# A fused Swin block and dynamic convolution: where operands are zeroed, who scales fc1, and the order of the first steps

## The chip, the cores and the metric

The kernel runs on one core of one Trainium2 chip. The metric is the device time in microseconds (us) of one execution, the median of several. Five engines work side by side, each through its own list of instructions in order: TensorE (PE in the profile, with its weight loads as PEld), VectorE (DVE), ScalarE (ACT), GpSimd (POOL) and SyncE (SP), which here only issues transfers. They wait for one another through semaphores. Transfers (DMA) are issued from the queues of SP, ACT and POOL.

## The reference, cut to what matters

The input is `x` (16, 192, 56, 56) in float32. Two layers follow each other. The first is a shifted-window attention block with an MLP, the second a depthwise 3x3 convolution whose taps are computed from the mean of its input.

```python
shortcut = x
h = _ln(transpose(x), norm1_g, norm1_b)          # over the 192 channels
h = roll(h, (-3, -3)); win = windows_7x7(h)      # 64 windows of 49 tokens an image
q, k, v = win @ qkv_w + qkv_b                    # 6 heads of 32
attn = softmax(q * SCALE @ k + rel_bias[REL_IDX] + mask)
out = attn @ v @ proj_w + proj_b
x1 = shortcut + unroll(out)
y = _ln(x1, norm2_g, norm2_b)
y = gelu(y @ fc1_w + fc1_b) @ fc2_w + fc2_b
x  = x1 + y                                      # end of layer 0
t  = relu(batchnorm(mean(x) @ w1.T))             # layer 1
wt = (t @ w2.T + b2) * MASK                      # only 4 of the 9 taps are left by MASK
out = depthwise_conv3x3(x, wt) + bias
```

## The kernel before

An image is worked on in four steps of two rows of windows each, so there are 64 steps (`NS`). A steady loop runs attention of step i, the MLP of step i - 2 and pieces of the convolution of finished images. Ahead of the loop stands a hand-ordered prologue (`manual_schedule`: each engine's instructions stand in the order in which the code emits them), which loads the weights, folds the norms' scale and mean into them, zeroes the padded operands and takes the attention of the first two steps. The change lies in this prologue alone. PSUM is used as four pairs of banks, taken with `banks(name, k)`.

The helpers that it touches:

```python
def columns(rows, n, name, k, copy):                 # rows of parameters to columns
    nc.vector.tensor_copy(rows[:, DIM:256], rows[:, C0:DIM])
    ...                                              # two transposes on TensorE, then copy()

def fold_scale(raw, g, dst, groups):                 # weight rows times the norm's gain
    for to, lo, n, factor in groups:
        for c in range(2):
            d, r = dst[:, c, to : to + n], raw[:, c, lo : lo + n]
            if factor == 1.0:
                nc.vector.tensor_scalar(d, r, g[c], None, ALU.mult)
            else:
                nc.vector.tensor_scalar(d, r, g[c], factor, ALU.mult, ALU.mult)

def shift(dst, raw, n, be, name):                    # the norm's offset through the weights
    ...
    row = one.tile([1, 2, n // 2], F32, tag="o", name=name)
    nc.scalar.copy(row, dst[0:1, :, : n // 2])

def norm_vars(keys, st, tag="dev"):                  # part = mean of squares - mean^2
    d = one.tile([128, T], F32, tag=tag, ...)
    nc.scalar.activation(part, st[lo:hi, 0, :T], AF.Square)
    nc.vector.tensor_tensor(part, st[64 + lo : 64 + hi, 0, :T], part, ALU.subtract)

def attention_qk(i, kq, ke, kk, between=None, evac=nc.scalar):
    for m in (0, 2, 1):
        short(dsts[m], ...)          # narrow products: 64 channels, win1
    if between:
        between()
    for m in (0, 1, 2):
        long(dsts[m], ...)           # wide products: 128 channels, win0
    ...
```

The prologue, cut to what the change and the prediction speak of:

```python
nc.vector.memset(rel_r, 0.0)
rows3 = columns_load(((norm2_g, 1), ...), "yn1", "cols2", nc.gpsimd)   # 5 DMAs of GpSimd
nc.sync.dma_start(mask_t, win_mask)                  # 113 partitions, last of SP's first loads
for j in range(2):
    for yq in range(WS):
        nc.gpsimd.dma_start(rel_r[...], ...)         # 14 DMAs of GpSimd
nc.gpsimd.memset(win0, 0.0)
nc.gpsimd.memset(win1, 0.0)
...
g1, be1, bq, bk, bv = columns(*rows1, 2, nc.vector.tensor_copy)
norm_squares("1_0", 0, 0, nc.scalar, ("yn0", "q4"))
fold_scale(raw, g1, wqkv, (...))                     # qkv, on VectorE
st = banks("st_a", 3); norm_stats(...)
part, _ = norm_vars(keys, st, "o")                   # tile of tag "o"
norm_root(part); nc.vector.reciprocal(part, part)
norm_squares("1_1", 1, 0, nc.scalar)
pm = fold_means(wqkv, 3 * DIM, "fq", 0)
row = shift(pq, raw, 3 * DIM, be1, "qkb_row")        # tile of tag "o" too
norm_squares("1_2", 2, 1, nc.scalar)
...                                                  # dv_0 (TensorE), fold_center, turn_row
g2, be2, f2b, pb, cb = columns(*rows3, 1, nc.scalar.copy)
norm1_scale(0, pd[:, :, :T], nc.vector)              # writes win0, win1
...
biases(0, 0)                                         # reads rel_r and mask_t, on VectorE
nc.gpsimd.memset(kbd, 0.0)
for t in vbd: nc.gpsimd.memset(t, 0.0)
for t in prob: nc.gpsimd.memset(t, 0.0)
st = banks("st_b", 0); norm_stats(...)
part, _ = norm_vars(keys, st); norm_root(part)
table(AF.Exp)
biases(0, 1)
...
qs[0], outs = attention_qk(0, 1, 2, 3)
pvs, v_rest, v_whole = attention_v(0, (0, 1))
for f in outs: f()
fold_scale(rawf, g2, wf1, ((0, 0, HID, 1.0),))       # fc1
attention_v_out(pvs)                                 # vbd, half on VectorE, half on ScalarE
norm1_scale(1, dvs.pop(0), nc.gpsimd)
...
norm1_scale(2, dvs.pop(1), nc.gpsimd)
pm = fold_means(wf1, HID, "ff", 1)                   # bank pair 1
top(2)
residual(0, pp, pair1)
norm_squares("2_0", 0, 1, nc.scalar)
st = banks("st_c", 0)
norm_stats(keys, {0: 3, 1: 0}, st)
qs[2], outs = attention_qk(2, 2, 1, 3, None, nc.vector)   # pe in bank pair 1
share(1)
fold_center(wf1, HID, pm)                            # reads bank pair 1
...
prts = [attention_turn(1, wp, (2, 3)[wp % 2]) for wp in range(4)]
```

Of the kernel before, what the change touches and what calls it, by code (L numbers as in the profile page):

```python
# [8 lines left out]
F32 = mybir.dt.float32  # L9
AF = mybir.ActivationFunctionType  # L10
# [26 lines left out]
def tile_swin_then_dynamic_conv(  # L37
# [112 lines left out]

    def fold_scale(raw, g, dst, groups):
        for to, lo, n, factor in groups:
            for c in range(2):
                d, r = dst[:, c, to : to + n], raw[:, c, lo : lo + n]
                if factor == 1.0:
                    nc.vector.tensor_scalar(d, r, g[c], None, ALU.mult)
                else:
                    nc.vector.tensor_scalar(d, r, g[c], factor, ALU.mult, ALU.mult)
# [15 lines left out]
    def shift(dst, raw, n, be, name):  # L174


        for c in range(2):
            cs = slice(c * n // 2, (c + 1) * n // 2)
            mm(dst[:, c, : n // 2], be[0].broadcast_to([128, 128]), raw[:, 0, cs], True, False)
            mm(  # L180
                dst[:, c, : n // 2],
                be[1][0:64].broadcast_to([64, 128]),
                raw[0:64, 1, cs],
                False,
                True,
            )
        row = one.tile([1, 2, n // 2], F32, tag="o", name=name)
        nc.scalar.copy(row, dst[0:1, :, : n // 2])
        return row.rearrange("o c n -> o (c n)")
# [65 lines left out]
    def table(func):  # L255

        nc.scalar.activation(junk, eps_t[0:1], func)  # L257
# [17 lines left out]
    def norm_folded(key, i, side):  # L275
# [11 lines left out]

        def sums():
            for p, h in own:
                nc.gpsimd.tensor_tensor(xs[p, 0], v0[p, h], v1[p], ALU.add)  # L290
            nc.gpsimd.tensor_tensor(xs[:, 0], xs[:, 0], xs[:, 1], ALU.add)

# [590 lines left out]
    side = 2 * WS - 1  # L883
    for j in range(2):
        for yq in range(WS):
            q = j * 64 + yq * WS
            nc.gpsimd.dma_start(
                rel_r[q : q + WS].rearrange("p (y x) h -> p y (x h)", y=WS),
# [4 lines left out]
                ),  # L893
            )
    nc.gpsimd.memset(win0, 0.0)
    nc.gpsimd.memset(win1, 0.0)
    rel_hk = rel_r[:, ::-1, :].rearrange("p k h -> p h k")

    def biases(r, e):
# [14 lines left out]

    g1, be1, bq, bk, bv = columns(*rows1, 2, nc.vector.tensor_copy)
    norm_squares("1_0", 0, 0, nc.scalar, ("yn0", "q4"))
    fold_scale(
        raw,
# [45 lines left out]
    biases(0, 0)  # L964
    nc.gpsimd.memset(kbd, 0.0)
    for t in vbd:
        nc.gpsimd.memset(t, 0.0)
    for t in prob:
        nc.gpsimd.memset(t, 0.0)

# [30 lines left out]
    for f in outs:  # L1001
        f()
    fold_scale(rawf, g2, wf1, ((0, 0, HID, 1.0),))
    attention_v_out(pvs)
    norm1_scale(1, dvs.pop(0), nc.gpsimd)
    w2v = w2.rearrange("(c t) r -> c t r", t=9)[:, 0:NTAP, :]
# [71 lines left out]
    keys = {0: "1_3", 1: "2_0"}  # L1078
    norm_stats(keys, {0: 3, 1: 0}, st)
    qs[2], outs = attention_qk(2, 2, 1, 3, None, nc.vector)  # L1080
    share(1)
# [4 lines left out]
    part, _ = norm_vars(keys, st)  # L1086
    table(AF.Sqrt)
    norm_root(part)

    s, m, g, b = (bn[:, k] for k in range(4))  # L1090
    nc.scalar.activation(s, s, AF.Sqrt, bias=eps_t)
    nc.vector.reciprocal(part, part)
    dvs.update(norm_spread(keys, part))
    outs[0]()
    outs[1]()
    prts = [attention_turn(1, wp, (2, 3)[wp % 2]) for wp in range(4)]
    outs[2]()
# [8 lines left out]
    table(AF.Gelu)  # L1106
    sums_()
    yns[0] = norm2_scale(0, dvs.pop(1), True)
    fold()
    attention_v_out(pvs)  # L1110
# [245 lines left out]
```

## Time and profile before

| What | Value |
|---|---|
| Device time, median of three | 3050.23 us (3049.95 to 3051.91) |
| Span of the profiled execution | 3046.8 us |
| TensorE busy | 3021.9 us (99%) |
| VectorE busy | 2156.5 us (71%) |
| ScalarE busy | 1947.1 us (64%) |
| GpSimd busy | 1345.4 us (44%) |
| TensorE busy in 0 to 100 us | 87.6 us |
| TensorE busy in 100 to 300 us | 200.0 us |

The busy time of TensorE is that between start and modelled end of its matmuls, so it says where TensorE had something in hand and not how well it was used. The last two rows come from the table of stretches of 20 us; they tell the prologue from the loop. The lines that the prediction reads are shown there.

### The profile page before, as it was taken

Reading aid. Unit: us, or ns where it says so; the run is one execution under the profiler, and the core shown is the slowest. Engines: PE = TensorE matmul, PEld = TensorE weight load, DVE = VectorE, ACT = ScalarE, POOL = GpSimd, SP = SyncE. Lnnn points to the kernel's source line nnn. Section 1 sums busy time; section 2 is a strip of 40 time slices with the busy share of each in tenths; the row PEclk is TensorE's granted clock in tenths of the full one; section 3 lists DMA queues with packets and bytes.
Section 4 is the critical chain, followed back from the end, with each engine's and each line's share of the span. In section 5 each row is a group of like instructions: output and inputs, shape, how many; then the busy total and the mean of one; then the engine's idle time right before and its main releaser. Section 6 shows DMA issues by size and latency. Waiting matters only on the chain.

```text
span 3046.8 us, 62149 instructions
## 1 busy us (share of the span) xinstructions
PE 3021.9 (99%) x25174; PEld 1892.6 (62%) x25174; DVE 2156.5 (71%) x3840; ACT 1947.1 (64%) x3159; POOL 1345.4 (44%) x1270
## 2 busy tenths in 40 slices
PE   8999999999999999999999999999999999999998
PEld 5666666666666666666666666666666666666654
DVE  8666676676676676766866767767767668667664
ACT  4665676676666666766756667667666666666563
POOL 6434544434435345444444354453444444543422
PEclk9999999999999999999999999999999999999999
DMA  4102121121211112121121211212111121111101
GB/s 111 33 31 59 41 68 45 42 65 44 75 38 62 52 44 67 39 78 35 42 67 47 70 36 52 65 41 77 39 44 59 46 73 38 62 52 43 33 30 56
DMA packets 68710, 159.87 MB, mean 52 GB/s; under 512 B 11250, under 2 KB 35288, under 8 KB 66504
## 3 DMA queue, kind: packets, MB, share of 16 engines
q1 hardware_dynamic: 66766, 153.84, 16.6%
q8 instruction: 198, 3.24, 0.4%
q0 software_dynamic: 1360, 1.26, 0.3%
q14 instruction: 88, 0.72, 0.1%
q10 hardware_dynamic: 298, 0.81, 0.1%
HBM read 92.24 MB, written 38.93 MB: 43 GB/s over the span
## 4 chain that ended last, share of the span: by engine, by line
PE 97%; DVE 1%; POOL 1%; DMA 0%; issue 0%; ACT 0%; POOLq 0%; DVEq 0%; ACTq 0%
PE ph L87 26%; PE pf L87 25%; PE pv L87 8%; PE pp L87 8%; PE po L87 6%; PE pq L87 5%; PE pt L575 5%; PE sc L87 4%; PE pk L87 4%; PE pe L87 4%; PE st L87 2%; PE pc L87 0%; DVE e L553 0%; DVE bias_t L905 0%; PE pb_p L87 0%
## 5 line engine op out<-in xcount | busy, mean ns | idle before, releaser
L87 PE MATMUL pf<-hid,wf 128*128 128x392 f32 (+1 forms) x3072 | 802.7, 494 | 1.5 <-DVE e L546 1.5
L87 PE MATMUL ph<-yn,wf 128*128 128x392 f32 (+1 forms) x3072 | 799.1, 497 | 0.3 <-DVE x L651 0.3
L562 POOL TENSOR_TENSOR prob<-e,tot 113x588 f32<-113x588 f32 x256 | 298.2, 1176 | 1096.8 <-DVE tot L561 1096.7
L87 PEld LDWEIGHTS ph<-yn,wf 128*128 128x128 f32 (+1 forms) x3072 | 427.0, 188 | 344.1 <-issue 46.9
L87 PEld LDWEIGHTS pf<-hid,wf 128*128 128x128 f32 (+1 forms) x3072 | 386.9, 164 | 300.7 <-issue 119.8
L518 ACT COPY vbd<-pv 49x192 f32<-49x192 f32 x512 | 160.1, 313 | 576.7 <-DVE vbd L518 572.2
L711 DVE SCALAR_TENSOR_TENSOR x<-pf,cols,x 128x784 f32<-128x784 f32 (+1 forms) x128 | 106.2, 830 | 507.2 <-PE pf L87 453.3
L665 ACT ACTIVATE hid<-ph,f1b 128x784 f32<-128x784 f32 x384 | 336.8, 913 | 134.1 <-PE ph L87 132.6
L775 DVE SCALAR_TENSOR_TENSOR y<-x,wt,y 128x770 f32<-128x770 f32 x282 | 287.3, 1028 | 15.3 <-ACT y L767 7.0
L87 PEld LDWEIGHTS pv<-wqkv,win 64*128 64x128 f32 (+1 forms) x2048 | 255.5, 189 | 30.7 <-issue 1.2
L87 PE MATMUL pv<-wqkv,win 64*128 64x192 f32 (+1 forms) x2048 | 272.2, 325 | 0.0
L553 DVE TENSOR_TENSOR e<-e,top 113x588 f32<-113x588 f32 x256 | 261.7, 1022 | 8.9
L290 POOL TENSOR_TENSOR xs<-x,x 64x392 f32<-64x392 f32 x246 | 249.0, 1012 | 34.7 <-DVE x L651 25.5
L87 PE MATMUL pp<-o,wp 128*128 128x392 f32 (+2 forms) x896 | 251.4, 514 | 0.0
L581 ACT COPY prt<-pt 128x678 f32<-128x678 f32 x256 | 179.2, 726 | 111.3 <-PE pt L575 109.8
L257 ACT ACT_TABLE_LOAD x192 | 246.3, 1283 | 5.2 <-issue 1.8
L556 ACT ACTIVATE e<-e 113x588 f32<-113x588 f32 x256 | 177.1, 692 | 110.9 <-DVE e L553 110.9
L546 DVE TENSOR_TENSOR e<-sc,bias_t 113x588 f32<-113x588 f32 x256 | 179.4, 762 | 60.7 <-PE sc L87 59.7
L411 POOL TENSOR_TENSOR yn<-x,dv 128x784 f32<-128x784 f32 x62 | 116.1, 1872 | 234.6 <-DMA dv<-rows 234.6
L575 PEld LDWEIGHTS pt<-ident,prob 113*128 113x128 f32 x1536 | 165.5, 141 | 65.5 <-issue 36.3
L87 PE MATMUL po<-prt,vbd 128*64 128x49 f32 x6144 | 197.1, 224 | 0.5 <-ACT prt L581 0.5
L87 PEld LDWEIGHTS po<-prt,vbd 128*64 128x64 f32 x6144 | 188.9, 138 | 9.7 <-ACT prt L581 0.6
(185 smaller groups left out, 4440.1 us busy)
## 6 DMA issues: line engine op xcount, KB each, us to landing
dv<-rows SPq DMA_DIRECT2D x127, 392.0 KB
xs<-x SPq DMA_DIRECT2D x246, 98.0 KB
x<-in_x_dram SPq DMA_DIRECT2D x15, 1484.0 KB
out_dram<-y SPq DMA_DIRECT2D x46, 392.0 KB
out_dram<-y SPq DMA_DIRECT2D x48, 196.0 KB
x<-in_x_dram SPq DMA_DIRECT2D x15, 392.0 KB
x<-in_x_dram SPq DMA_DIRECT2D x15, 350.0 KB
out_dram<-y SPq DMA_DIRECT2D x16, 308.0 KB
```

The costliest lines, as they stand in the source:

```text
L87: nc.tensor.matmul(dst, lhs, rhs, start=start, stop=stop, skip_group_check=True)
L257: nc.scalar.activation(junk, eps_t[0:1], func)
L290: nc.gpsimd.tensor_tensor(xs[p, 0], v0[p, h], v1[p], ALU.add)
L518: copy(dst, src[s * 64 : s * 64 + N, h, :, :, j, :])
L546: nc.vector.tensor_tensor(e, sc[:PW, :, : HEADS * N], rel, ALU.add)
L553: nc.vector.tensor_tensor(ehs[wp], ehs[wp], t.broadcast_to([PW, 2 * HEADS, N]), ALU.subtract)
L556: nc.scalar.activation(es[wp], es[wp], AF.Exp)
L562: nc.gpsimd.tensor_tensor(prob[wp][:PW, :, 0:N], ehs[wp], t.broadcast_to([PW, 2 * HEADS, N]), ALU.mult)
L575: nc.tensor.transpose(pt[:, a, g * PW : (g + 1) * PW], prob[wp][:PW, h : h + 2, :].rearrange("p h k -> p (h k)"), ident[:PW, :PW],)
L581: nc.scalar.copy(prt, pt[:, :, : 3 * PW])
L665: nc.scalar.activation(hid[:, f], phs[f][:, :, :T], AF.Gelu, bias=f1b[:, f : f + 1])
L775: nc.vector.scalar_tensor_tensor(dst, src, wt[:, kc, t : t + 1], dst, ALU.mult, ALU.add)
```

## The change

Six things are moved, and no arithmetic of the result is changed.

1. The zero fills leave their place behind `biases(0, 0)`. `prob` and `vbd` are zeroed on GpSimd directly behind its first transfers; `kbd` is zeroed on VectorE, in the stretch in which that engine waits for the qkv weights.
2. The fourteen loads of the relative bias table are divided: seven stay on GpSimd's queue, behind the fills of `win0` and `win1`, and seven go to ScalarE's queue, behind the squares of step 0.
3. The row in which the shifted offsets are collected uses the buffer of tag "xs" and no longer that of tag "o", which holds the deviations at that time.
4. fc1 is scaled on ScalarE by an activation with a per-partition scale, behind the evacuation of V and not ahead of it.
5. In step 2, the statistics (`st_c`) are put between the narrow and the wide products of Q, K and E; the root follows the evacuation of Q.
6. In step 1, the turned probabilities use the bank pairs 2 and 0, where they used 2 and 3, and the root of the batch norm moves behind them. The sums of step 4's folded norm are divided, with the second norm's scaling between them.

```diff
--- before.py
+++ after.py
@@ -148,11 +148,13 @@
 
 
 
-    def fold_scale(raw, g, dst, groups):
+    def fold_scale(raw, g, dst, groups, engine=nc.vector):
         for to, lo, n, factor in groups:
             for c in range(2):
                 d, r = dst[:, c, to : to + n], raw[:, c, lo : lo + n]
-                if factor == 1.0:
+                if engine is nc.scalar:
+                    nc.scalar.activation(d, r, AF.Copy, scale=g[c])
+                elif factor == 1.0:
                     nc.vector.tensor_scalar(d, r, g[c], None, ALU.mult)
                 else:
                     nc.vector.tensor_scalar(d, r, g[c], factor, ALU.mult, ALU.mult)
@@ -184,7 +186,7 @@
                 False,
                 True,
             )
-        row = one.tile([1, 2, n // 2], F32, tag="o", name=name)
+        row = one.tile([1, 2, n // 2], F32, tag="xs", name=name)
         nc.scalar.copy(row, dst[0:1, :, : n // 2])
         return row.rearrange("o c n -> o (c n)")
 
@@ -285,10 +287,12 @@
             nc.sync.dma_start(xs[0:64, 1], v0[64:128, 0])
             nc.sync.dma_start(xs[64:128, 1], v0[0:64, 1])
 
-        def sums():
-            for p, h in own:
-                nc.gpsimd.tensor_tensor(xs[p, 0], v0[p, h], v1[p], ALU.add)
-            nc.gpsimd.tensor_tensor(xs[:, 0], xs[:, 0], xs[:, 1], ALU.add)
+        def sums(parts=(0, 1)):
+            if 0 in parts:
+                for p, h in own:
+                    nc.gpsimd.tensor_tensor(xs[p, 0], v0[p, h], v1[p], ALU.add)
+            if 1 in parts:
+                nc.gpsimd.tensor_tensor(xs[:, 0], xs[:, 0], xs[:, 1], ALU.add)
 
         def squares(engine):
             def those_of(dst, src):
@@ -881,10 +885,11 @@
     nc.sync.dma_start(mask_t, win_mask)
 
     side = 2 * WS - 1
-    for j in range(2):
+
+    def rel_load(j, queue):
         for yq in range(WS):
             q = j * 64 + yq * WS
-            nc.gpsimd.dma_start(
+            queue.dma_start(
                 rel_r[q : q + WS].rearrange("p (y x) h -> p y (x h)", y=WS),
                 bass.AP(
                     rel_bias.tensor,
@@ -892,8 +897,12 @@
                     [[HEADS, WS], [side * HEADS, WS], [1, WS * HEADS]],
                 ),
             )
+
     nc.gpsimd.memset(win0, 0.0)
     nc.gpsimd.memset(win1, 0.0)
+    rel_load(0, nc.gpsimd)
+    for t in (*prob, *vbd):
+        nc.gpsimd.memset(t, 0.0)
     rel_hk = rel_r[:, ::-1, :].rearrange("p k h -> p h k")
 
     def biases(r, e):
@@ -913,7 +922,9 @@
 
 
     g1, be1, bq, bk, bv = columns(*rows1, 2, nc.vector.tensor_copy)
+    nc.vector.memset(kbd, 0.0)
     norm_squares("1_0", 0, 0, nc.scalar, ("yn0", "q4"))
+    rel_load(1, nc.scalar)
     fold_scale(
         raw,
         g1,
@@ -962,11 +973,6 @@
     nc.vector.tensor_scalar(qkb[0:64, 2:3], qkb[0:64, 2:3], SCALE, None, ALU.mult)
     nc.vector.tensor_scalar(kb, pick, qkb[:, 1:2], None, ALU.mult)
     biases(0, 0)
-    nc.gpsimd.memset(kbd, 0.0)
-    for t in vbd:
-        nc.gpsimd.memset(t, 0.0)
-    for t in prob:
-        nc.gpsimd.memset(t, 0.0)
 
 
     st = banks("st_b", 0)
@@ -1000,8 +1006,8 @@
     v_whole()
     for f in outs:
         f()
-    fold_scale(rawf, g2, wf1, ((0, 0, HID, 1.0),))
     attention_v_out(pvs)
+    fold_scale(rawf, g2, wf1, ((0, 0, HID, 1.0),), nc.scalar)
     norm1_scale(1, dvs.pop(0), nc.gpsimd)
     w2v = w2.rearrange("(c t) r -> c t r", t=9)[:, 0:NTAP, :]
     b2v = b2.rearrange("(c t) -> c t", t=9)[:, 0:NTAP]
@@ -1076,8 +1082,9 @@
     norm_squares("2_0", 0, 1, nc.scalar)
     st = banks("st_c", 0)
     keys = {0: "1_3", 1: "2_0"}
-    norm_stats(keys, {0: 3, 1: 0}, st)
-    qs[2], outs = attention_qk(2, 2, 1, 3, None, nc.vector)
+    qs[2], outs = attention_qk(
+        2, 2, 1, 3, lambda: norm_stats(keys, {0: 3, 1: 0}, st), nc.vector
+    )
     share(1)
     fold_center(wf1, HID, pm)
     top(3)
@@ -1085,15 +1092,15 @@
     share(3)
     part, _ = norm_vars(keys, st)
     table(AF.Sqrt)
+    outs[0]()
     norm_root(part)
+    nc.vector.reciprocal(part, part)
+    dvs.update(norm_spread(keys, part))
+    outs[1]()
+    prts = [attention_turn(1, wp, (2, 0)[wp % 2]) for wp in range(4)]
 
     s, m, g, b = (bn[:, k] for k in range(4))
     nc.scalar.activation(s, s, AF.Sqrt, bias=eps_t)
-    nc.vector.reciprocal(part, part)
-    dvs.update(norm_spread(keys, part))
-    outs[0]()
-    outs[1]()
-    prts = [attention_turn(1, wp, (2, 3)[wp % 2]) for wp in range(4)]
     outs[2]()
     outs[3]()
     o = attention_rows(1, attention_values(1, prts, 2, 3))
@@ -1104,8 +1111,9 @@
     copies()
     squares(nc.scalar)()
     table(AF.Gelu)
-    sums_()
+    sums_((0,))
     yns[0] = norm2_scale(0, dvs.pop(1), True)
+    sums_((1,))
     fold()
     attention_v_out(pvs)
     pp, pair1, p_narrow, p_rest, p_whole = project(1, o, 3, 2)
```

## The prediction

> **What bounds the kernel now.** I read the page first: TensorE's busy time, then the chain that ended last.
>
> ```profile
> PE 3021.9 (99%) x25174; PEld 1892.6 (62%) x25174; DVE 2156.5 (71%) x3840; ACT 1947.1 (64%) x3159; POOL 1345.4 (44%) x1270
> PE 97%; DVE 1%; POOL 1%; DMA 0%; issue 0%; ACT 0%; POOLq 0%; DVEq 0%; ACTq 0%
> ```
>
> TensorE is the bound, and the table of stretches says where it is not: busy 87.6 us of the first 100, then 200.0 of the next 200. The change touches the prologue alone, so at most the 12.4 idle us, plus matmuls that run at a low clock, are to be had. TensorE is full from about 100 us on, so a prologue that is shorter by d should end the kernel d earlier; what other engines save counts only as far as it moves TensorE. I then read the timeline of each engine over 0 to 100 us. The longest hole of TensorE after its start, and what lies behind it, in the timelines of VectorE, GpSimd and TensorE (start, duration, engine, line, what; in brackets the idle time before):
>
> ```profile
> 16.02 6.42 DVE L138 COPY cols_rows<-cols_rows 5x64 f32<-5x64 f32 x1
> 17.02 5.42 DVE L387 TENSOR_TENSOR win<-x,dv 128x343 f32<-128x343 f32 x2
> ```
>
> ```profile
> 13.60 0.97 POOL L895 MEMSET win<- 128x1024 f32 x1
> 14.49 0.54 POOL L896 MEMSET win<- 128x512 f32 x1
> 14.96 2.08 POOL L965 MEMSET kbd<- 128x2352 f32 x1
> 16.95 2.72 POOL L967 MEMSET vbd<- 128x1536 f32 x2
> 19.59 2.80 POOL L969 MEMSET prob<- 128x768 f32 x4
> ```
>
> ```profile
> 22.50 0.26 PE L141 MATMUL cols_p<-ident,cols_rows 5*128 5x5 f32 x1 [3.35 <-DVE win L395]
> 22.69 0.87 PE L87 MATMUL st_b<-x,sel 128*32 128x392 f32 x2
> ```
>
> A copy of 64 columns takes 6.42 us; its like at 3.90 takes 0.23. It ends at 22.44, just after GpSimd's row of zero fills (22.39). TensorE's second transpose waits for it. The clock, by stretches of 2 us:
>
> ```profile
> 18.00:20.00 2.00, 1.14 (x12) 0.99 (x11) 2.00 (x4) 0.75 (x2) 2.00 (x3) 0.73 0.36 92
> 20.00:22.00 2.00, 0.00 (x0) 0.00 (x0) 2.00 (x4) 0.00 (x0) 2.00 (x4) 0.50 0.07 23
> 24.00:26.00 2.00, 2.00 (x20) 0.59 (x12) 1.54 (x13) 0.00 (x0) 2.00 (x5) 0.57 0.22 58
> ```
>
> The last figures are clock, DMA share and GB/s: half speed from about 19 to 25.7, so `st_b` takes 3.6 us (22.69 to 26.28).
>
> [...] the copy got in at none of the six borders between the fills from `kbd` on. [...] the trace has 111 packets at 24 GB/s between 18.9 and 22.6 us, the mask's, on a queue that moved 220 before.
>
> **The change, part by part.**
>
> *Zero fills.* On GpSimd the order becomes five small loads (to 4.11 as now), fills of `win0`, `win1` (1.4), seven bias loads (7 x 0.59 = 4.1), `prob` and `vbd` (2.8 + 2.7): fills from 9.7 to about 15.3, or 16.3 if they first wait for VectorE's scaling (8.99 to 10.78). `kbd` on VectorE: 2352 elements at the 0.8 ns each of its other fills (294 in 0.30) is 1.95 us, from 4.66 to 6.6, ahead of the scaling at 7.79. [...] 6.2 us of VectorE's wait gone. Its four large window products start 0.42 apart (17.02 to 17.87), the small ones take 1.2.
>
> *Bias loads on ScalarE.* Here I see a cost that the change does not intend. In the built instruction streams the transfers of SP and ScalarE take eight semaphores in turn, and each waits until the last user of its semaphore has landed. ScalarE's squares end at 5.95. Its third load waits for the first qkv weight load (VectorE saw it at 7.79), the fourth for the last (8.99), the fifth for the second, the sixth for a load of `x`, the seventh for the fourth. An early load of ScalarE was issued at 1.54 and used at 3.90, so landing takes about 2.4: the seventh goes out near 8.95 + 2.5 = 11.5, and ScalarE is free at 12.0. But the mean square of `st_a` stands behind it, and began at 9.35. From 12.0: 0.48, VectorE 0.56, root 0.62, reciprocal 2.59 and small waits give 16.4 (now 14.65), `dv` on TensorE to 18.0, windows 18.1 + 4 x 0.42 + 1.25 = 21.0 (now 24.26).
>
> *The row's tag.* The row waited until `dv` had read the deviations (16.95). It is now ready before `dv` ends, which takes out TensorE's wait of 0.72.
>
> *TensorE in step 0.* `dv` to 18.0, turned rows 1.3, transposes 0.4, `st_b` from 19.7. I take most of it at half clock, 3.3 us: the first narrow product at about 23.0, 3.2 earlier than 26.28.
>
> *The mask.* `biases(0, 0)` needs it. It landed at 22.7 and the biases began at 25.59, so it cost nothing. Now VectorE arrives at 21.0 + 0.95 + 0.4 for semaphores = 22.4. With ScalarE's loads among the eight semaphores SP issues the mask a little later, so I put it at 23.2, and the six biases at 23.4 to 24.9. Behind them stands the subtraction of `st_b` (27.12 before): 2.2 earlier. From there 2.8 us to the evacuation of Q on ScalarE (27.7 instead of 30.14), then 6.3 without the 0.7 of waits it had: 34.0 instead of 36.82, when the scores may start. So of TensorE's 3.2 us about 2.75 are left.
>
> *fc1.* VectorE loses 1.13 us (34.67 to 35.80). The copies of V start at 35.82, but the first half of V is complete at about 35.8 too (32.61 + three quarters of 4.3). The move alone gives nothing; with the mask it keeps VectorE from being last. ScalarE gets about 2 x 0.86 and has 3.1 idle there.
>
> *Step 2.* The idea is to fill TensorE's 0.54 us in front of the squares:
>
> ```profile
> 74.56 0.52 PE L87 MATMUL st_c<-sq,sel 128*32 128x392 f32 x1 [0.54 <-ACT sq L268]
> ```
>
> ```profile
> 73.81 0.53 POOL L395 TENSOR_TENSOR win<-x,dv 64x21 f32<-64x21 f32 x2
> ```
>
> ```profile
> 74.47 1.75 DVE L172 TENSOR_TENSOR wf<-wf,ff_m 128x768 f32<-128x768 f32 x2
> ```
>
> The narrow products need the windows, whose last piece ends at 74.34, and `pe` lies in bank pair 1, which `fold_center` still reads until 76.22. In the old clock: wait to 74.4, `pq` 0.7, wait to 76.3, `pe` and `pk` 1.4, `st_c` 2.1, wide products 4.15: 83.9 instead of 83.05. That costs 0.9.
>
> *Turned tiles of step 1.* `pt` waited 0.59 and 0.30 and `po` 0.50. Bank pair 0 is free early, so the second tile need not wait for K. ScalarE's chain (Q, root, K, then four copies of 0.73) ends at 88.2, and `po`, 2.97 us, runs from 87.4 to 90.4, as before (90.37). The gain of some 1.0 pays for the loss of 0.9. The root comes 2.1 us later and so `dv` (VectorE used it at 89.94) at 92, but its products are wanted at 98.35.
>
> **Sum.** -2.75 in step 0, 0.0 in steps 1 and 2: 3050.2 - 2.7 = 3047.5.
>
> **Rivals.** (a) *The mask is early, ScalarE is not held*: ScalarE's loads go out in a row (0.25 to 0.5 each) by 9.4. The windows are then done near 20.0 and TensorE gains 5, if the mask lets it; I expect the mask at 22.7 or later, which leaves 3.2 and 3047. Without that limit: 3045. For it: loads of 8 KB are small. Against: GpSimd stands 1.1 us on the same kind of wait now. (b) [...] VectorE waits until 15.3. The qkv fold comes 5 us late: 3052. Against: VectorE's scalings overlap (0.20 apart, 0.29 long), as GpSimd's fills did when they kept the copy out. (c) *Step 2 works as meant*, if `fold_center` comes earlier there: another 0.8, 3046.5. (d) *Cold clock*: if TensorE stays at half speed until 25.7, half of the narrow products is slow too, and 1.2 less is gained: 3048.7.
>
> **Range and chances.** (a) and (c) pull to 3045, (d) and a later mask to 3049, (b) beyond 3051; with the spread of the kernel before (3049.95 to 3051.91) I take 3045.0 to 3050.5. Nothing here reaches 2% (61 us), since the prologue has 12.4 us of idle TensorE and some 3 us of slow clock: within 2% at 0.98, 0.01 for either side.
>
> **What would show it.** The copy at L138 in 0.25 us and no hole of 3 us before the second transpose. ScalarE's mean square near 12 and not 9.4, with waits among its seven loads. `biases` beginning at 23 to 23.6 by a wait on a transfer. `pq` near 23. In step 2, TensorE waiting twice, for GpSimd's windows and for `fold_center`. The loop unchanged, 20.00 of 20 busy. I am wrong if the copy still waits, if the mean square starts before 10, or if the loop loses the lead again.

## The result and the profile after

The changed kernel takes 3058.24 us (median of 6 runs, 3057.29 to 3060.45) against 3050.09 us (3048.56 to 3051.91) for the kernel before: a ratio of 1.0028, 95% interval 1.0015 to 1.0041. It is slower by some 8 us, and the range of the prediction (3045.0 to 3050.5) missed it. The profiled execution spans 3055.5 us against 3046.8, and the difference is complete when the loop begins: the first product of the MLP (`ph`) starts at 106.74 us instead of 98.35, 8.39 later. So the loop is unchanged, and the search is confined to the first 100 us. TensorE before and after:

```profile
98.35 2.14 PE L87 MATMUL ph<-yn,wf 128*128 128x392 f32 x6
```

```profile
106.74 3.46 PE L87 MATMUL ph<-yn,wf 128*128 128x392 f32 x10
```

Some names of tiles come up again and again. `st_a`, `st_b` and `st_c` are TensorE's sums for the statistics of a norm. `fq_m` and `qkb_p<-raw` are the products that fold the norm into the qkv weights (the fold). `dv` is the reciprocal deviations, spread over the partitions; the windows `win` are made with them. `pq`, `pe` and `pk` are the products that give Q, E and K. A lead is how much earlier TensorE starts a product than in the kernel before.

First the timeline of VectorE after, where the change was meant to help. Columns as before: start, duration, engine, line, operation, operands, count, and in brackets the idle time ahead and what ended it.

```profile
3.93 1.66 DVE L138 COPY cols_rows<-cols_rows 5x64 f32<-5x64 f32 x1 [1.45 <-DMA cols_rows<-in_L_conv_qkv_b_dram]
...
8.49 6.73 DVE L160 TENSOR_SCALAR wqkv<-raw,cols 128x128 f32<-128x128 f32 x2
15.13 0.50 DVE L158 TENSOR_SCALAR wqkv<-raw,cols 128x128 f32<-128x128 f32 x2
...
22.29 0.17 DVE L138 COPY cols_rows<-cols_rows 5x64 f32<-5x64 f32 x1
```

The copy that took 6.42 us before now takes 0.17: the aim was reached. But two scalings of the qkv weights, begun at 8.49, aren't done until 15.2. Their like took 0.29 each before:

```profile
8.99 0.29 DVE L158 TENSOR_SCALAR wqkv<-raw,cols 128x128 f32<-128x128 f32 x1 [0.92 <-DMA raw<-in_L_conv_qkv_w_dram]
```

The timeline of GpSimd after shows beside what they stand:

```profile
4.11 0.97 POOL L901 MEMSET win<- 128x1024 f32 x1
5.00 0.54 POOL L902 MEMSET win<- 128x512 f32 x1
...
9.63 2.79 POOL L905 MEMSET prob<- 128x768 f32 x4
12.35 2.72 POOL L905 MEMSET vbd<- 128x1536 f32 x2
```

The scalings end just behind the last fill of `vbd` (15.22 and 15.07). The small copy at 3.93, too, ends just behind the fills of `win` (5.59 and 5.54), which delays the first statistics (`st_a`) by 1.45 us. And the timeline of TensorE, before and after:

```profile
9.89 2.79 PE L87 MATMUL fq_m<-wqkv,ones 128*128 128x288 f32 x8 [0.57 <-DVE wqkv L158]
12.61 2.79 PE L87 MATMUL qkb_p<-raw,cols 128*128 128x288 f32 x8
15.33 1.58 PE L87 MATMUL dv<-dev,ident 32*128 32x392 f32 x4
...
26.28 0.93 PE L87 MATMUL pq<-win,wqkv 64*128 64x392 f32 x4
```

```profile
15.82 5.09 PE L87 MATMUL fq_m<-wqkv,ones 128*128 128x288 f32 x8 [5.03 <-DVE wqkv L160]
20.84 5.10 PE L87 MATMUL qkb_p<-raw,cols 128*128 128x288 f32 x8
25.87 1.01 PE L87 MATMUL dv<-dev,ident 32*128 32x392 f32 x1
...
34.20 0.93 PE L87 MATMUL pq<-win,wqkv 64*128 64x392 f32 x4
```

There are two losses here, not one. The fold starts 5.93 us late. Then it also runs at nearly half its pace: `fq_m` and `qkb_p` take 5.1 us each, where they took 2.8. The clock by stretches of the kernel after (the last three figures are clock, DMA share, GB/s):

```profile
10.00:16.00 6.00, 0.97 (x3) 0.18 (x2) 6.00 (x7) 0.48 (x1) 6.00 (x8) 0.80 0.66 174
16.00:22.00 6.00, 6.00 (x10) 2.31 (x10) 4.91 (x8) 1.89 (x3) 5.35 (x10) 0.50 0.88 208
22.00:30.00 8.00, 8.00 (x24) 4.19 (x24) 1.51 (x5) 1.80 (x3) 0.54 (x1) 0.50 0.29 24
30.00:34.00 4.00, 4.00 (x26) 1.16 (x26) 3.66 (x23) 0.17 (x1) 0.00 (x0) 0.50 0.01 2
34.00:40.00 6.00, 6.00 (x27) 3.24 (x24) 5.64 (x13) 4.19 (x6) 0.00 (x0) 0.99 0.01 3
```

By the profile TensorE was busy all the time from 16 us on, and yet the clock stayed at half until 34.06, 20.5 us in all from 13.58. Up to the first narrow product of step 0 (`pq`) the account is therefore: fold late 5.93, fold slow 4.61 (from 5.44 us to 10.05), everything from `dv` to the start of `st_b` 3.03 shorter (the hole of 3.35 and the wait of 0.72 are gone, half clock takes back a part), `st_b` 0.41 longer: 7.92 together, 34.20 instead of 26.28. Steps 1 and 2 add 0.47.

ScalarE's timeline after shows the hold that the prediction had worked out:

```profile
6.43 6.09 ACTq L892 DMA_DIRECT2D rel_r<-in_L_conv_rel_bias_dram  x7
12.56 0.48 ACT L349 ACTIVATE dev<-st_a 32x392 f32<-32x392 f32 x1 [5.68 <-DMA rel_r<-in_L_conv_rel_bias_dram]
```

The mean square is at 12.56 (predicted 12.0, 9.35 before). But VectorE takes it up at 16.74 only, so the hold costs nothing here. And TensorE's waits in step 2 after, summed by the table of waits over 70 to 105 us:

```profile
PE pe L87 <- DVE wf L174: 1.1, 1, 1.1
PE pt L579 <- ACT prt L585: 0.9, 1, 0.9
PE pq L87 <- POOL win L399: 0.9, 1, 0.9
PE po L87 <- ACT prt L585: 0.2, 1, 0.2
```

The two waits in step 2 are the ones that the prediction named (windows, `fold_center`).

### The profile page after: what moved, and what is told of

Read it like the earlier page. It is cut to its first block, busy times and chain, and to the rows that moved or that the text cites. A ratio compares the mean times of both kernels' runs of the same rounds, so it can differ in the third digit from the quotient of the medians.

```text
span 3055.5 us, 62149 instructions
## 1 busy us (share of the span) xinstructions
PE 3027.5 (99%) x25174; PEld 1893.8 (62%) x25174; DVE 2161.4 (71%) x3839; ACT 1948.7 (64%) x3161; POOL 1339.7 (44%) x1262
## 4 chain that ended last, share of the span: by engine, by line
PE 98%; DVE 1%; issue 0%; DMA 0%; ACT 0%; SPq 0%; POOL 0%; POOLq 0%; DVEq 0%; ACTq 0%
PE ph L87 26%; PE pf L87 25%; PE pv L87 8%; PE pp L87 8%; PE po L87 6%; PE pq L87 5%; PE pt L579 5%; PE sc L87 4%; PE pe L87 4%; PE pk L87 4%; PE st L87 2%; PE pc L87 0%; DVE wqkv L160 0%; PE qkb_p L87 0%; DVE e L557 0%; PE pb_p L87 0%
## 5 line engine op out<-in xcount | busy, mean ns | idle before, releaser
L779 DVE SCALAR_TENSOR_TENSOR y<-x,wt,y 128x770 f32<-128x770 f32 x282 | 287.9, 1030 | 15.3 <-ACT y L771 7.0
```

The costliest lines, as they stand in the source:

```text
L779: nc.vector.scalar_tensor_tensor(dst, src, wt[:, kc, t : t + 1], dst, ALU.mult, ALU.add)
```

## The experiments

Thirteen kernels were run. Since steps of less than 1 us are lost in the spread of the times, I also read where TensorE stands at four places of the profiled execution (us): the start of the fold, of `pq` in steps 0 and 1, and of `ph`. "Time" is the median with its range; the kernel before had 3049.0 to 3049.1 beside them.

| Kernel | fold | pq, step 0 | pq, step 1 | ph | time |
|---|---|---|---|---|---|
| before | 9.89 | 26.28 | 43.70 | 98.35 | 3050.09 (3048.56 to 3051.91) |
| after | 15.82 | 34.20 | 51.77 | 106.74 | 3058.24 (3057.29 to 3060.45) |
| e1_rel_sp | 15.84 | 34.30 | 51.98 | 107.46 | 3057.76 (3056.81 to 3060.14) |
| e2_one_port | 10.40 | 22.43 | 43.00 | 98.60 | 3055.28 (3049.46 to 3058.37) |
| e3_warm | 15.93 | 26.00 | 45.53 | 103.76 | 3053.11 (3051.06 to 3054.66) |
| e4_copy_act | 9.57 | 22.28 | 41.98 | 98.11 | 3049.05 (3047.04 to 3052.27) |
| e5_steps12 | 9.55 | 26.12 | 44.04 | 99.57 | 3050.30 (3048.57 to 3052.50) |
| e6_mask | 10.78 | 21.64 | 41.86 | 98.67 | 3049.28 (3047.25 to 3050.93) |
| e7_before_best | 9.74 | 21.24 | 42.76 | 103.45 | 3048.60 (3045.58 to 3053.79) |
| e8_first_act | 9.09 | 24.40 | 41.98 | 97.06 | 3048.70 (3047.03 to 3050.34) |
| e9_loads | 10.12 | 20.27 | 40.23 | 95.39 | 3046.92 (3045.69 to 3048.14) |
| e10_loads_steps | 9.31 | 19.47 | 40.04 | 96.03 | 3045.50 (3044.43 to 3047.40) |
| e11_loads_warm | 9.83 | 20.10 | 42.39 | 96.66 | 3048.68 (3047.25 to 3053.33) |
| e12_best_warm | 9.94 | 21.55 | 42.50 | 96.78 | 3048.69 (3046.84 to 3052.07) |
| e13_late_dense | 19.56 | 29.61 | 49.04 | 106.94 | 3056.14 (3053.62 to 3060.14) |

Theory A: GpSimd's fills keep VectorE's scalings out, the hole drops TensorE's clock, and the fold at half clock cannot bring it back. Rival B: ScalarE's held mean square sets the pace. Rival C: the new order of steps 1 and 2 is what costs.

### e1_rel_sp: ScalarE's loads moved to SP

```diff
-    rel_load(1, nc.scalar)
+    rel_load(1, nc.sync)
```

> The changed kernel with the seven bias loads of ScalarE moved to SyncE's queue; the zero fills stay where the change put them. [...] (the fills of prob and vbd, from 9.6 us on, keep VectorE's scaling of the qkv weights out until 15.2): nothing is won, scaling ends near 16.7, first fold product at 15.8, 3057 to 3059. Rival, ScalarE held by its own loads: the mean square of st_a begins near 10.8 instead of 12.6 and the kernel comes back to 3048 to 3050.

Ratio to before 1.0031 (1.0020 to 1.0042), as the changed kernel. The fold stays at 15.84, again after a wait for VectorE's scaling, now of 4.54. The mean square came at 11.34 instead of 12.56, and nothing was won by it. Rival B falls for this kernel; the hold is real but lies beside a longer wait.

### e2_one_port: the scaling as another instruction

Same arithmetic, other instruction: the gain comes as a second operand from SBUF and not as a per-partition scalar.

```diff
-                elif factor == 1.0:
-                    nc.vector.tensor_scalar(d, r, g[c], None, ALU.mult)
                 else:
-                    nc.vector.tensor_scalar(d, r, g[c], factor, ALU.mult, ALU.mult)
+                    gain = g[c].broadcast_to([128, n])
+                    nc.vector.scalar_tensor_tensor(d, r, factor, gain, ALU.mult, ALU.mult)
```

> The changed kernel with the qkv scaling written so that the gain is a second operand read from SBUF for each element (scalar_tensor_tensor)[...]; the same values, fills and loads unmoved. [...] the scaling runs from 8.5 to some 10.6 beside the fills, the fold products begin near 10.6 at full clock, ScalarE's hold then sets the rest as the prediction had it, and the time is 3046 to 3049. If the operation is shut out as well[...]: 3057 to 3059 as before.

Ratio 1.0017 (1.0008 to 1.0026), with times from 3049.5 to 3058.4: the time that I expected was missed, the start of the fold was not. VectorE's timeline in the profiled run:

```profile
8.50 1.91 DVE L159 SCALAR_TENSOR_TENSOR wqkv<-raw,cols 128x128 f32<-128x128 f32 x10
...
25.45 1.49 DVE L913 TENSOR_TENSOR bias_t<-rel_r,mask_t 113x98 f32<-113x98 f32 x6 [3.11 <-DMA mask_t<-in_win_mask_dram]
26.97 0.57 DVE L349 TENSOR_TENSOR dev<-st_b,dev 64x392 f32<-64x392 f32 x1
```

The fills stand where they did (9.64 to 15.08), but the scaling isn't held: it begins at 8.50, where it began in the changed kernel too, and all ten instructions are done at 10.41, the last of them beside the first fill. The fold starts at 10.40 at full clock and `pq` at 22.43, 3.85 ahead of the kernel before. So it was the hold of these instructions that made the hole. Why the one instruction is held beside fills and the other isn't, no run shows. By the records the held scalings began at 8.49, 1.1 us ahead of the first fill, while GpSimd was still issuing loads; why they were held all the same stays open (starts on GpSimd are rough in the profile). The issuing alone isn't it: in the kernel before, the scalings at 7.79 and 8.99 took 0.29 us each while GpSimd issued loads (4.11 to 9.45).

The lead is then gone at step 1 (43.00). The second line says where: VectorE stood 3.11 us for the mask, so the deviations of `st_b`, which TensorE had finished at 22.4, were taken up at 26.97. What the fold's delay had covered in the changed kernel (biases at 33.14) now binds.

### e3_warm: the hole filled, the delay left

```diff
+    idle = banks("idle", 1)
+    for _ in range(7):
+        mm(idle[:, 0, :T], ones, flat_of(0)[0][:, 0], True, True)   # read by nobody
     pm = fold_means(wqkv, 3 * DIM, "fq", 0)
```

> The changed kernel with seven products more (128x128 by 392, never used) in TensorE's hole between st_a and the fold; all waits stay. It measures what the low clock is worth. If the clock doubles the damage: fold products from 15.8 at 0.34 us each instead of 0.64, first narrow product of step 0 near 27 instead of 34.2, 3050 to 3052. If the 6 us [...] are all there is: 3057 to 3059.

Ratio 1.0013 (1.0006 to 1.0020), some 5 us below the changed kernel. TensorE's timeline:

```profile
11.21 4.88 PE L87 MATMUL idle<-x,ones 128*128 128x392 f32 x14
15.93 2.70 PE L87 MATMUL fq_m<-wqkv,ones 128*128 128x288 f32 x8
...
18.56 2.79 PE L87 MATMUL qkb_p<-raw,cols 128*128 128x288 f32 x8
...
26.00 1.04 PE L87 MATMUL pq<-win,wqkv 64*128 64x392 f32 x4
```

The fold is as late as in the changed kernel (15.93), and `pq` is 8.2 us earlier than there, because the clock did not fall ahead of it. The data and the weight loads are the same, so the slow fold is a matter of the clock alone. With the clock up, `pq` is also level with the kernel before (26.28): what the change gains behind the fold makes up for the late start, and the whole 7.92 us at `pq` is what the clock took. Later the lead over the changed kernel shrinks from 8.2 to 3.0 at `ph`: 2.1 go up to step 1's scores, 2.2 where the clock falls in step 2 (76.0 to 82.8), and 0.8 ahead of `ph`.

### e4_copy_act: the kernel before, its held copy on ScalarE

```diff
-    def columns(rows, n, name, k, copy):
-        nc.vector.tensor_copy(rows[:, DIM:256], rows[:, C0:DIM])
+    def columns(rows, n, name, k, copy, first=nc.vector.tensor_copy):
+        first(rows[:, DIM:256], rows[:, C0:DIM])
-    g2, be2, f2b, pb, cb = columns(*rows3, 1, nc.scalar.copy)
+    g2, be2, f2b, pb, cb = columns(*rows3, 1, nc.scalar.copy, nc.scalar.copy)
```

> The kernel before with one edit: the second copy of 64 columns of parameter rows goes to ScalarE[...]. [...] the hole of 3.35 us before the second transposes closes, the windows of step 0 are done near 20.0, and with the mask landing at 22.7 the first narrow product comes near 23; 3046 to 3048.5. Rival, the hole has another cause: 3050.

The same aim as the change, without moving a fill. The hole of 3.35 us is gone and `pq` comes 4.00 earlier; the time is that of before (ratio 1.0002, 0.9993 to 1.0011). Of the 4.00, 2.3 are lost by step 1's `pq` and 1.5 more at 53.53 to 56.95, where the clock fell once more. VectorE's timeline:

```profile
16.70 0.93 DVE L387 TENSOR_TENSOR win<-x,dv 128x343 f32<-128x343 f32 x2 [0.92 <-PE dv L87]
...
20.58 1.18 DVE L963 TENSOR_SCALAR kb<-pick,qkb 128x2 f32<-128x2 f32 x1
22.34 1.47 DVE L905 TENSOR_TENSOR bias_t<-rel_r,mask_t 113x98 f32<-113x98 f32 x6 [0.59 <-DMA mask_t<-in_win_mask_dram]
```

and GpSimd's beside it:

```profile
16.29 2.72 POOL L967 MEMSET vbd<- 128x1536 f32 x2
18.93 2.80 POOL L969 MEMSET prob<- 128x768 f32 x4
```

This completes the reading of the kernel before: the window products (`tensor_tensor`) run freely beside fills (0.93 us for two), while a `tensor_scalar` of two columns waits until 21.7 (1.18; in e2_one_port, with no fill beside it, 0.21). In the kernel before, the windows were late because they stood behind the copy in VectorE's queue.

### e5_steps12: parts 5 and 6 alone

The kernel before with the change's order of steps 1 and 2 and its divided sums; nothing else.

> The kernel before with parts 5 and 6 of the change alone (order of step 2 and of step 1's turned tiles, divided sums); parts 1 to 4 undone. My theory: between the start of pq and the loop the changed kernel lost 0.5 us more, and this comes from step 2, where TensorE waits twice (GpSimd's windows 0.86, fold_center 1.05) and gets back less in step 1. So: every product up to the fold of fc1 (69.9 us) starts where it did before, ph starts 0.4 to 0.7 later than 98.35, and the time is 3050.6 (3049.8 to 3051.2). Rival (the sum in the prediction): loss 0.9 and gain 1.0 cancel, ph at 98.3, time as before, 3050.0. Second rival: these parts carry more than 2 us of the loss by a stretch at half clock in step 2, time 3052 or more.

Ratio 1.0004 (0.9996 to 1.0012): the time does not resolve it. The positions do: 0.65 us behind at the second scores and 1.22 behind at `ph`, so 0.57 is lost in between. In the changed kernel the same stretch loses 0.57, in e8_first_act 0.68. Rival C explains some 0.6 of 8 us. A second cost showed later (e9_loads).

### e6_mask, e7_before_best, e8_first_act: where the leads go

e6_mask is e2_one_port with the mask divided. In the kernel before, the packets between 18.9 and 22.6 us, the mask's, moved 24 GB/s and took 7.7% of the time of 16 DMA engines, as much as 1.2 of them have; what kept them to so few, no trace shows.

```diff
-    nc.sync.dma_start(mask_t, win_mask)
+    nc.sync.dma_start(mask_t[0:112], win_mask[0:112])
+    nc.sync.dma_start(mask_t[112:PW], win_mask[112:PW])
```

> The changed kernel with the scaling [...] (as in e2_one_port), and the window mask loaded in two transfers, of 112 and of 1 partition. My theory of where the 3.9 us went that the first products of step 0 had gained in e2_one_port: VectorE stood 3.11 us for the mask (biases began at 25.45, so the root of st_b, GpSimd's windows and step 1 came late). [...] the mask lands by about 21.5, biases begin at 22.4 as VectorE arrives there, step 1's narrow products (pq) start near 40.5 instead of 43.0, and the profile's span is 3045 or less where TensorE's clock is as in that profile. The times stay widely spread, 3047 to 3056, because the spread has another cause (clock). Rival: the mask is late for another reason [...] (it is issued late, or queues behind the other loads), lands at 24 or later, and pq of step 1 stays near 43.

VectorE's timeline, where the biases begin:

```profile
23.58 1.47 DVE L914 TENSOR_TENSOR bias_t<-rel_r,mask_t 113x98 f32<-113x98 f32 x6 [0.89 <-DMA w1n<-in_L_conv_w_dram]
```

They begin 1.9 us earlier (the transfer in the brackets is inferred; the biases read only the bias table and the mask), the wait falls from 3.11 to 0.89, and step 1's `pq` stands at 41.86 (I expected 40.5). The time is level with before: ratio 0.9999 (0.9991 to 1.0007). The wide spread of e2_one_port went too, against my expectation.

e7_before_best is the kernel before with e4's copy, the divided mask, and parts 3 and 4 of the change.

> The kernel before with four small steps: its second copy of parameter rows on ScalarE (as in e4_copy_act), the row's other tag and fc1 scaled on ScalarE (parts 3 and 4 of the change), and the mask in two transfers of 112 and 1 partitions. Zero fills and bias loads stay as before. In e4_copy_act the lead of 4.0 us at pq fell to 1.7 at step 1's narrow products, since VectorE waited 0.59 us for the mask and then had fc1 in its way, and to 0.24 by half clock over 53.5 to 57. My theory: pq of step 0 near 21.6, TensorE's wait of 0.72 gone, pq of step 1 at 40.3 to 41.3, and the time 3047.3 (3045.5 to 3049.5); with a spell of half clock in step 1 some 1.5 more. Rival: GpSimd's windows are bound by something else, pq of step 1 stays at 42 or later and the time at 3049.

Ratio 0.9997 (0.9989 to 1.0005). The best run is 3045.58 at a mean clock of 0.999, the worst two are 3053.6 and 3053.8 at 0.996; the profiled one is among these two and shows why. TensorE and, below, SP's transfers of the deviations (`dev` to `rows` to `dv`):

```profile
42.76 1.98 PE L87 MATMUL pq<-win,wqkv 64*128 64x392 f32 x4 [3.42 <-POOL win L397]
```

```profile
27.60 0.58 SPq L357 DMA_DIRECT2D rows<-dev  x1
31.97 0.82 SPq L364 DMA_DIRECT2D dv<-rows  x2
```

A lead of 4.91 us at the scores falls to 0.94 by a wait of 3.42 for GpSimd's windows, which need `dv`; and after this wait the clock is at half from 42.03 to 55.68, so that `ph` is 5.1 late. `dv<-rows` waits until `rows` has landed, 4.4 us after its issue here, and 1.7 in e8_first_act and e10_loads_steps. In e7 GpSimd issues its loads of weights and statistics until 28.6, behind the fills; in the other two it is done by 23. Over all 15 traces the time from `rows` to `dv` is 1.7 us in the twelve in which GpSimd was done with these loads at least 2.8 us ahead of `rows`, and 2.41, 3.26 and 4.37 in the three in which it wasn't (e12, e4, e7). That these loads delay `rows` fits, but no run takes them away alone.

e8_first_act is e6_mask with both copies of parameter rows on ScalarE.

> e6_mask with both copies of parameter rows on ScalarE. The first of them took VectorE 1.66 us instead of 0.23 beside the fills of win, so st_a began 1.45 us later than before and lasted only some 3.5 us. My theory of the wide spread of e2_one_port (3049.5 to 3058.4): [...] the clock stays at half through the fold and until st_b. [...] times within 3 us of each other, near 3046 (3044.5 to 3048), mean clock 0.998 or more in every run. Rival: the spread comes from later spells (step 1 or 2), then it stays as wide as in e6_mask, with clocks of 0.994 to 0.996 in some runs.

Ratio 0.9997 (0.9989 to 1.0006), times within 3.3 us. The theory behind it fell: e6_mask begins `st_a` as late as e2_one_port, and has no wide spread either. In e2_one_port the longer runs have a lower mean clock (0.994 to 0.997 from 3055.1 us on, 0.998 or 0.999 below 3052.5); a spell as in e7 would do that, but the one trace that there is shows a run of 3050.2, so the cause stays open. `pq` of step 0 came only at 24.40: now ScalarE's hold does bind (TensorE waits 2.1 for `dv`).

### e9_loads and e10_loads_steps: the change repaired

e9_loads is the changed kernel with e2's scaling, both copies on ScalarE, and the order of SP's transfers below; e10_loads_steps undoes parts 5 and 6 as well.

```diff
-    rel_load(1, nc.scalar)
+    # on SP: x, mask in two transfers, these seven loads, then the fc1 weights
+    rel_load(1, nc.sync)
+    nc.sync.dma_start(rawf[:, 0], fc1_w[0:C0])
+    rows2(rawf[:, 1], fc1_w, nc.sync)
```

> The changed kernel with four repairs: the scaling [...], both copies of parameter rows on ScalarE, the mask in two transfers issued ahead of the fc1 weights, and the seven bias loads of ScalarE moved to SP behind the mask. What held e8_first_act back was the mean square of st_a, which stood behind those seven loads until about 12, and the mask, which VectorE awaited until 24.0. My theory: mean square at 9.4, dv of step 0 at 14.8 without a wait, first narrow product (pq) near 22, biases at 20.6 to 21.5, the transfer of the deviations not behind other loads, step 1's pq at 39 to 40 (43.70 in the kernel before), ph at 95 to 96.5 where the clock stays up, time 3046.5 (3044.5 to 3049). Rival: a wait takes their place (the bias loads on SP land late, or the deviations' transfer is slow), step 1's pq at 41.5 or later and the time no better than the 3048.7 of e8_first_act.

> e9_loads with parts 5 and 6 of the change undone (steps 1 and 2 in the order of the kernel before). Those parts cost 0.57 us between the scores of step 1 and the loop in e5_steps12, 0.57 in the changed kernel and 0.68 in e8_first_act. My theory: the same up to the fold of fc1, then 0.6 earlier than e9_loads at ph; time 0.6 below e9_loads, which the spread of the times may hide. Rival: with the windows of step 2 earlier the new order pays as it was meant to, and e10_loads_steps is level with e9_loads or later at ph.

e9_loads has 0.9993 (0.9985 to 1.0001). e10_loads_steps has 0.9988 (0.9981 to 0.9994): 3.5 us faster than the kernel before, and the one version here whose interval lies wholly below 1. Its TensorE timeline:

```profile
9.31 2.79 PE L87 MATMUL fq_m<-wqkv,ones 128*128 128x288 f32 x8 [0.35 <-DVE wqkv L159]
12.04 2.79 PE L87 MATMUL qkb_p<-raw,cols 128*128 128x288 f32 x8
...
19.47 1.04 PE L87 MATMUL pq<-win,wqkv 64*128 64x392 f32 x4
```

`pq` is 6.8 us earlier than before. By step 1 it is 3.7. In e9_loads TensorE waits 0.65 there for GpSimd's windows; here they last from 32.86 to 39.7, and half clock from 35.43 to 42.26 took another 1.4 behind that place. So this profile is 0.64 behind that of e9_loads at `ph`, against my expectation; the medians have it the other way. In the 3.4 us ahead of this fall TensorE waits 0.83 and 0.74 us for the copies of V.

Parts 5 and 6 cost 0.58 in e9_loads, between 66 and 98 us (lead 3.54 to 2.96). The medians differ by 1.4. That is more, and traces of three other kernels with these parts show a second cost: behind the double wait of step 2 the clock fell in e3_warm (76.0 to 82.8), e6_mask (75.1 to 78.5) and e13_late_dense (79.6 to 86.4). It stayed up there in the other six profiled kernels with the new order, and fell in none of the six with the old one. That this makes up the difference of the medians isn't shown.

### e11_loads_warm, e12_best_warm: idle products in step 1

Four products as in e3 ahead of step 1's `pq`, in e10 and in e7.

> e10_loads_steps with four idle products of 128x128x392 (their result is read by nobody) ahead of step 1's narrow products, where TensorE waits for GpSimd's windows. My theory: this wait is what drops the clock in step 1 in some runs (38.6 to 52.3 in the trace of e7_before_best, whose lead of 4.9 us became a loss of 5.1), so the slow tail of the times goes: all within 2.5 us of each other, median 3045.5 (3044 to 3047.5). Rival: the spells come from elsewhere (the one-column products and turned tiles at 50 to 57), then the tail stays, or the products only push pq back and the median is no better.

> e7_before_best with the same four idle products ahead of step 1's narrow products. There TensorE waited 3.4 us for GpSimd's windows and the clock went to half for 13.7 us. My theory (the clock falls after a window of 3.41 us with little streaming, and comes back only after one that is nearly full): no half clock between 38 and 53, the times above 3050 disappear, median 3047 (3045.5 to 3049) against 3048.6 (3045.6 to 3053.8) without them. Rival: the clock falls for another reason, and the times keep a tail to 3053.

Both ratios are 0.9998 (0.9990 to 1.0006). In both profiles the clock stays up between 30 and 75 us, so they do what they were for. (In e7 the clock fell at 42.03, after the wait; the expectation for e11 puts the spell 3.4 us too early.) Yet e11's median lies 3.2 us above that of e10, with one run at 3053.33. I had taken 0.33 us for such a product; they take 0.66 (2.90 us for the four), where e10 had less than 1 us to wait, and they push `pq` from 40.04 to 42.39. In e12 the times reach 3052 all the same. Two of its runs, 3046.84 and 3052.07, have the same mean clock of 0.998. Its rounding leaves room for some 6 us at half clock, or 3 us of time (an estimate from the span), so half clock can hardly be the only cause of that tail.

### e13_late_dense: the clock down, then dense products

What was still open: is it the fold that cannot raise the clock, or does it need time? Here the hole stays; five products follow the mean square on TensorE, ahead of the fold, and delay it.

```diff
+    mm(idle[:, 1, :T], ident[64:96, 64:65].broadcast_to([32, 128]), part, True, True)
+    for _ in range(5):
+        mm(idle[:, 0, :T], ones, flat_of(0)[0][:, 0], True, True)   # read by nobody
     ...                                         # ahead of fold_means(wqkv, ...)
```

> The changed kernel with its hole left in place: TensorE stands idle until ScalarE's mean square is done (about 13 us), so that the clock falls, and then runs five products of 128x128x392 that nobody reads, densely, straight ahead of the fold of qkv. They delay the fold: at half clock each takes 1.3 us, so it starts at 18 to 19.6 instead of 15.82. My theory (the clock falls after a window of 3.41 us with little streaming and comes back only after a nearly full one; the fold's chain, which streams some 3/4 of the time at half clock, keeps a clock that is up but cannot bring it back): the clock is up when the fold starts or soon after, fq_m and qkb_p take 2.8 us each instead of 5.1, and pq starts at 29 to 31 instead of 34.2, though the fold starts later. Time 3054 (3051.5 to 3056.5) against 3058.2. Rival: the fold is slow in the changed kernel for a reason of its own (VectorE's or GpSimd's late data, weight loads), or the clock comes back with time alone; then it takes 5 us each again or the extra products just add their length, pq at 36 to 38 and a time of 3060 or more.

```profile
13.62 0.92 PE L87 MATMUL idle<-dev,ident 32*128 32x392 f32 x2 [2.33 <-ACT dev L945]
14.47 5.25 PE L87 MATMUL idle<-x,ones 128*128 128x392 f32 x10
19.56 2.69 PE L87 MATMUL fq_m<-wqkv,ones 128*128 128x288 f32 x8
22.18 2.79 PE L87 MATMUL qkb_p<-raw,cols 128*128 128x288 f32 x8
...
29.61 1.04 PE L87 MATMUL pq<-win,wqkv 64*128 64x392 f32 x4
```

The fold starts 3.7 us later than in the changed kernel and `pq` 4.6 us earlier. The clock fell at 14.75, the products raised it at 18.16, and the fold kept it up. So it is not time: in the changed kernel the fold ran for 10 us at half clock without raising it. There the last window of 3.41 us at full clock streamed columns for 0.10 of its time, the two windows wholly in the fold for 0.75 and 0.78, and the one ahead of 34.06, which full clock follows, for 1.00 (last section). The time, 3056.14 (ratio 1.0025, 1.0016 to 1.0034), keeps only 2 of the 4.6 us. In the profiled execution (3057.26) all of it is gone at `ph`: 2.0 go up to step 1's scores (TensorE waits 0.82 for the copies of V and 0.65 for GpSimd's windows), 2.3 where the clock falls in step 2, and 0.5 ahead of `ph`.

## Why the prediction was wrong

**Zero fills: the step that failed.** That the copy would not wait is right (0.17 us at 22.29). But beside the same fills, moved to 9.63 to 15.07, the qkv scalings took until 15.2. The prediction had this as rival (b), with the wait until 15.3 (15.2 measured) and the fold 5 us late (5.9), and set it aside because "VectorE's scalings overlap". Overlap among VectorE's own instructions was no protection: the first two stood beside the fills together (6.73 us for both). What decides here is which instruction it is, and e2 shows it by changing that alone: ten scalings in 1.91 us, and the fold at 10.40 instead of 15.82. It was also overlooked that the copy at 3.93 meets the fills of `win` (1.66 us). So the fill of `kbd` ran from 6.55 to 8.57, not from 4.66 to 6.6, and the first scaling came at 8.49 instead of 7.79. Of the three signs that the prediction named for being wrong (the copy waits, the mean square starts before 10, the loop loses a lead) none came.

**Clock: rival (d), mis-sized by far.** It allowed 1.2 us. Rival (b) put the whole at 3052 by the delay alone, and e3_warm, with the delay and the clock up, has 3053.11. The other 5 us are the clock, which fell in a hole of 5 us and which the fold did not raise. The prediction took (b) and (d) one at a time, but (b) brings (d) about. e3 and e13 show this from both sides: with the clock up, `pq` is 8.2 earlier at the same start of the fold, and 4.6 earlier at a later one. I had taken it that the clock comes back once TensorE is busy again. That was too coarse: by the profile TensorE was busy for 18 us at half clock, from 15.82 to 34.06.

**Bias loads on ScalarE.** Right (12.56 against 12.0), hidden in the changed kernel, and binding where the scalings aren't held (e8: TensorE waits 2.1 for `dv`).

**Row's tag.** Right: no wait ahead of the turned rows.

**TensorE from `dv` to `st_b`.** The intended gain came. From the end of `dv` to `st_b` 5.78 us became 1.35, where 1.7 was predicted. `dv` itself took 1.40 longer at half clock, so 3.03 remain from its start. They are covered by the losses ahead of it.

**Mask.** Right in kind, mis-sized: biases could begin at 25.45 (e2), not 23.4. In the changed kernel nothing waits for it.

**fc1.** That the move alone gives nothing was tried only together with other steps, so it stays open.

**Steps 1 and 2.** Both waits of step 2 are there, 0.86 and 1.05 us. Step 2 loses 1.17 (predicted 0.9), the turned tiles gain 0.60 (predicted 1.0): 0.57 lost instead of nothing. That the clock can fall there was not foreseen.

**The loop.** Right: 8.39 at `ph` is 8.7 at the end. And "within 2%" held: 8 us are 0.3%.

## What to carry to other kernels

When an operand is zeroed "in an idle stretch", look at what the other engines do in that stretch, instruction by instruction: here the fills that were moved away from a copy (6.42 us before, 0.17 after) held two scalings instead (0.29 us for one before, 6.73 for two after). Where TensorE waits, count the clock with the wait: here a gap of 5.0 us cost the fold behind it another 4.6. And a lead won early is worth only what the next late transfer or engine leaves of it: of 4.0 us at `pq` e4_copy_act had 0.2 left at `ph`, and of 6.8 us e10_loads_steps had 2.3.

## What the hardware showed beyond that

The clock changes lie on a grid of 3.41 us in every trace: half clock lasts 6.83 us in the kernel before (18.91 to 25.74, two windows) and 20.48 in the changed kernel (13.58 to 34.06, six). To see what moves it, I counted for each such window from 3 to 105 us, in all 15 traces, the share of time in which columns stream (392 columns last 0.65 us at half clock and 0.33 at full, by the spacing of `st_b`). In the kernel before, the last window at full clock has 0.34, the two at half clock 0.00 and 0.90, and full clock follows. In the changed kernel the last one at full clock has 0.10, the six at half clock 0.28, 0.75, 0.78, 0.68, 0.52 and 1.00.

Of 58 windows at half clock in all traces, 31 are followed by full clock; their share is 0.82 to 1.00. Of the other 27, all but one lie at 0.84 or below (the one at 0.89). The windows that lie wholly in a fold at half clock have 0.74 to 0.79. At full clock the same fold has some 0.7 and keeps it; the 16 windows after which the clock fell have 0.61 or less, and the lowest that kept it 0.43. So in these runs the clock came back only with a higher share (0.82 or more) than some with which it stayed up (0.43 or more). The lower figure isn't sharp in this count: 8 windows below 0.43 all lost the clock, but between 0.43 and 0.61 only 8 did and 70 kept it. What tells these apart stays open.

Where the grid lies against a kernel differs from trace to trace (13.58 and 18.91 lie 1.56 windows apart). Whether that makes the times scatter (e2: 9 us, e7: 8 us; the kernel before: 3 us) isn't shown, with one trace for each kernel.
